# Moving the small steps of expert routing to other engines, and shifting attention's streams in the planned order

## The chip, the cores and the metric

The kernel runs on one core of a Trainium2 chip. The metric is device time in microseconds (us) of one execution, as the median of several runs. Besides, one execution is recorded by the hardware profiler; its busy times, waits and timelines are what this document reads.

Engines are named as in the profile: PE (TensorE), DVE (VectorE), ACT (ScalarE), POOL (GpSimd) and SP (SyncE, which issues most of the DMAs). [...]

## What is computed

Eight images (x is 8 x 512 x 256, the context 8 x 1024 x 192) go through two blocks. The first is a cross-attention whose scores keep the 32 largest of 1024 per row and head, followed by a state-space convolution with film modulation and a GELU MLP. The second is a mixture of experts: each token goes through a shared expert and through the one of 8 routed experts with the largest gate logit. Cut to what matters here:

```
scores = einsum('bthd,bghd->bhtg', Q, K) / sqrt(DH)
topv, topi = top_k(scores, 32)
attn = zeros.at[..., topi].set(softmax(topv)); attn_mean = attn.mean(axis=1)
c_t = attn_mean @ V            # feeds film, the convolution, the MLP
...
logits = x @ gate_w
top_val = max(logits); top_id = argmax(logits)
xs = x * sigmoid(top_val)
y = silu(xs @ rt_gate[e]) * (xs @ rt_up[e]) @ rt_down[e]   # e = top_id
out = swiglu(x, sh_gate, sh_up, sh_down) + y
```

## The kernel before, in words

**Streams.** The work of each image b is written as generators. `prepare(b)` (line 434) loads x and the context, normalises, and makes the transposed keys and queries kT and qT. `attention` (905) is one generator over all images: 64 steps, each one 128-row tile and two heads. `scores` (890) multiplies queries and keys on PE into PSUM and copies the result on ACT into two `sc` tiles (pool pq, four buffers, so two steps' worth); it is called one step ahead. A step then makes pairwise maxima and minima (`mn`, on DVE and POOL), finds the 32nd largest by repeated MAX8 and MATCH_REPLACE8 on DVE, takes Exp on ACT, masks on DVE, and sums heads into `acc` on POOL. After four heads `weighted` (872) transposes acc on PE (`pa`) and multiplies with the context (`pu`) into uT. `mixed(b)` (1053) does film and convolution (xm, pxf, yf, py, xr); `after_mix(b)` (1095) does the MLP (pm, ga, am), the norms, routing, and the shared expert (p, sg, ge, ae). `routed` runs routed-expert blocks of 128 rows (xb, pg, pu, ger, pyr), loading the weights of the expert that a block belongs to. While attention of image b runs, `behind(b - 1)` (1365) runs the rest of image b - 1, with the routed blocks of image b - 2 in it, and `prepare(b + 1)` runs too. Image 7's own rest, with 15 routed blocks, has no attention beside it.

**Routing** (1150 to 1184, once per image). The gate logits `lg` are copied from PSUM; DVE finds the largest (mx) and its index (ix) for each of four row tiles. The index is cast to a float (fx) and compared with iota8 to a one-hot oh (128 x 4 x 8). A row's place within its expert's table is the count of earlier rows of that expert. `cum`, 128 x 5 x 8, carries running one-hot sums: four dependent additions per image. Two small matmuls into one PSUM bank, before16 (a strict triangle of ones) by oh and ones16 by cum, give the ranks pw; pw times oh summed over experts, plus fx times CAP, is the row number, cast to ix_, and four indirect DMAs on POOL's queue scatter the rows into a table in DRAM (xtab). The sigmoid of the largest logit (sg_) scales the rows on ACT before that.

**blocks_of** (1213, images 1 to 7) turns counts into a list of (expert, first row) of blocks that are full: a matmul of ones16 by cum (pcnt), then some twenty tiny DVE operations on 128 x 8 tiles (nb, pre, base, di, pdone, cm, rd) up to the integer list `blk`, which SP's queue reads before it loads a block's weights. In the last image it lists all that remain.

**The order.** All calls go through a planner (class Plan). `note` and `time` give each operation a cost in us; `add` (179) numbers it and sets its priority `op.k = op.i - self.lead` in line 181 (a smaller k goes first); `order` (218) simulates the five engines and always issues, on the engine that can begin first, the available operation with the smallest k. Whatever comes out is the fixed order of each engine's queue. `ahead` (307) runs one step of a generator with `lead` set: LEAD_A for attention, LEAD_P for preparation, both 0. Where the plan has PE idle, `busy` (1394) puts in filler matmuls, `idle`.

## Time and profile before

| | |
|---|---|
| runs | 1898.41 us median of 3 (1895.82 to 1899.57) |
| profiled execution | 1896.74 us, span of instructions 1895.0 us |
| granted TensorE clock | 0.949 |
| busy: PE, DVE, ACT, POOL | 1727.0, 1483.8, 1187.0, 1043.7 us |
| PE filler matmuls `idle` | 397.2 us, 1574 of them |
| first `mn` of images 1 to 7 | 287.6, 465.8, 649.6, 835.5, 1024.4, 1221.2, 1418.7 us |
| last masked product of attention on DVE | ends at 1621.4 us |

How to read the lines: a group or timeline line names start and duration (us), engine, source line, operation and `output<-inputs` with shapes. Nearly every operation has line L324, the planner's issue line, so one goes by tile names. A table of stretches gives the stretch, its length, then for PE, weight loads, DVE, ACT and POOL the busy us with the count in brackets, then the granted clock, the DMA share and GB/s. A line of waits gives the waiting engine and tile, what released it, the total in us, the number of times and the longest. The strips cut the span into 40 slices; each digit is busy tenths.

### The profile page before, as it was taken

The numbers are of one execution on the slowest core, as the hardware profiler recorded it, in microseconds if no ns is written. First come the engines' busy times: TensorE is split into PE (matmuls) and PEld (weight loads), VectorE is DVE, ScalarE is ACT, GpSimd is POOL, SyncE is SP. The second block draws the span as 40 slices with busy tenths as digits, with TensorE's granted clock in tenths as the row PEclk, the third lists the DMA queues.
The fourth block names the chain that finished last, engine by engine and source line by source line (L and its number), as shares of the span: only waits on it lengthen the run. The fifth ranks groups of instructions, "written<-read, shape, count | busy, mean of one in ns | idle before, by whom it ended". The sixth has DMA issues, their size and how long they took to land. (4 is left out here: it accounts for less than half of the span.)

```text
span 1895.0 us, 24257 instructions
## 1 busy us (share of the span) xinstructions
PE 1727.0 (91%) x7913; PEld 998.3 (53%) x7913; DVE 1483.8 (78%) x2975; ACT 1187.0 (63%) x2022; POOL 1043.7 (55%) x916
## 2 busy tenths in 40 slices
PE   7598997989998999989899899989998999899996
PEld 3254443435543554556447453755465546657685
DVE  4999997897989899879998989888988999431210
ACT  6577753478757875977578657965696659513221
POOL 6454353665656657584655657465747665532122
PEclk9799997989989999989999899989998999999998
DMA  4000110001200120134004220323023302642594
GB/s 111 1 1 12 41 35 17 1 12 45 67 17 12 56 79 11 35 111 140 1 12 142 74 68 12 112 64 108 12 70 106 92 1 71 205 156 75 176 288 134
DMA packets 101302, 131.89 MB, mean 70 GB/s; under 512 B 9687, under 2 KB 73004, under 8 KB 101166
## 3 DMA queue, kind: packets, MB, share of 16 engines
q1 hardware_dynamic: 93102, 121.05, 20.8%
q0 software_dynamic: 7008, 8.42, 2.5%
q8 instruction: 65, 1.06, 0.2%
q10 hardware_dynamic: 1056, 0.79, 0.1%
q14 instruction: 71, 0.58, 0.1%
HBM read 112.22 MB, written 18.78 MB: 69 GB/s over the span
## 5 line engine op out<-in xcount | busy, mean ns | idle before, releaser
L1396 PE MATMUL idle<-ones 128*128 128x512 bf16 x1574 | 397.2, 397 | 0.0
L324 POOL TENSOR_TENSOR mn<-sc 128x512 int32<-128x512 int32 x128 | 203.1, 1600 | 223.6 <-DVE top L324 165.9
L324 POOL TENSOR_TENSOR acc<-acc,e 128x1024 f32<-128x1024 f32 x96 | 233.8, 2436 | 86.1 <-ACT e L324 80.1
L1396 PEld LDWEIGHTS <-ones 128*128 128x128 bf16 x1574 | 153.2, 102 | 238.8 <-issue 104.8
L324 DVE MAX8 top<-left 128x8 f32<-128x512 f32 x384 | 265.9, 692 | 11.3
L324 PE MATMUL pS<-kT,qT 32*128 32x512 f32 x512 | 199.6, 668 | 36.9 <-ACT sc L324 35.7
L324 DVE SCALAR_TENSOR_TENSOR e<-sc,t,e 128x1024 f32<-128x1024 f32 x128 | 215.9, 1709 | 10.7 <-ACT e L324 10.0
L324 POOL TENSOR_TENSOR mn<-mn 128x512 int32<-128x512 int32 x128 | 176.4, 1389 | 81.3 <-DVE mn L324 78.5
L324 ACT ACT_TABLE_LOAD x139 | 178.3, 1283 | 5.5 <-issue 2.0
L324 ACT COPY sc<-pS 128x512 f32<-128x512 f32 x256 | 140.3, 583 | 63.2 <-PE pS L324 62.0
L324 DVE MAX8 top<-mn 128x8 f32<-128x512 f32 x256 | 169.2, 678 | 10.6 <-POOL mn L324 10.5
L324 DVE MATCH_REPLACE8 left<-top,left 128x512 f32<-128x512 f32 x256 | 172.9, 676 | 0.0
L324 ACT ACTIVATE e<-sc,sm 128x1024 f32<-128x1024 f32 x128 | 147.0, 1149 | 8.8 <-POOL acc L324 3.9
L324 ACT ACTIVATE junk<-sc,sm 128x1024 bf16<-128x1024 f32 x128 | 146.1, 1142 | 1.6
L324 DVE TENSOR_TENSOR mn<-sc 128x512 f32<-128x512 f32 x128 | 117.3, 945 | 14.2 <-ACT sc L324 14.2
L324 PEld LDWEIGHTS pu<-aT,cx 128*96 128x96 f32 x1024 | 115.7, 163 | 16.2 <-ACT aT L324 7.0
L324 PE MATMUL pu<-aT,cx 128*96 128x128 f32 x1024 | 120.7, 273 | 3.7 <-ACT aT L324 2.8
L324 PE MATMUL am<-w,ga 128*128 128x256 f32 x512 | 117.9, 382 | 0.8 <-ACT ga L324 0.7
L324 PE MATMUL pm<-hT,w 128*128 128x512 f32 x256 | 117.9, 596 | 0.5 <-ACT hT L324 0.2
L324 PEld LDWEIGHTS pS<-kT,qT 32*128 32x128 f32 x512 | 56.9, 190 | 112.7 <-ACT sc L324 69.5
L324 POOL DMA_INDIRECT out_dram<-yb,to x38 | 65.9, 1735 | 84.8 <-DMA out_dram<-yb,to 47.7
L324 ACT ACTIVATE e<-e,sm 128x1024 f32<-128x1024 f32 x96 | 107.6, 1141 | 7.2 <-DVE sm L324 7.2
(266 smaller groups left out, 3153.1 us busy)
## 6 DMA issues: line engine op xcount, KB each, us to landing
rt_gate<-in_L_ffn_rt_gate_dram SPq DMA_DIRECT2D x38, 512.0 KB, 4.8
rt_up<-in_L_ffn_rt_up_dram SPq DMA_DIRECT2D x38, 512.0 KB, 3.7
rt_down<-in_L_ffn_rt_down_dram SPq DMA_DIRECT2D x38, 512.0 KB, 4.1
w<-in_L_xattn_W_dram SPq DMA_DIRECT2D x32, 512.0 KB, 4.3
cx<-in_ctx_dram SPq DMA_DIRECT2D x7, 768.0 KB
xtab<-zt SPq DMA_DIRECT2D x8, 642.5 KB, 4.8
xb<-xtab SPq DMA_DIRECT2D x38, 128.5 KB, 4.2
xt<-in_x_dram SPq DMA_DIRECT2D x8, 512.0 KB, 4.4
```

The lines of the kernel that those rows point to most:

```text
L324: o.fn()
L1396: nc.tensor.matmul(idle, ones16, bc(ones16, 1, 4), start=True, stop=True)
```

## The change

It does four things. (1) The planner's costs change: indirect DMAs on POOL 1.15 us, with accumulation 1.7 (both 1.1 before); ACT operations at least 0.24 us, and 0.16 more for 129 to 256 elements from SBUF. (2) Leads: attention and preparation get -100, and `scores` adds 150 while it notes its operations. (3) Routing's small operations go to an engine E: POOL for images 0 to 6, DVE for image 7. The cum chain goes: `cum` becomes 128 x 8 and holds only the total of earlier images; ranks come from five matmuls, before16 by oh, ones16 by oh shifted by one, two and three tiles, and ones16 by cum broadcast. DVE sums oh over tiles (om), and E adds that to cum. (4) In blocks_of the scaling of the counts is a copy from PSUM on ACT, and most other operations go to E; two multiply-adds become two instructions each, because the tile minimum, the comparison, the reduction and the final minimum alone stay on DVE.

```diff
--- before.py
+++ after.py
@@ -117,7 +117,7 @@
         if dma:
             moved = out if kw.get("out_offset") is None else kw["in_"]
             size = self.width(moved) * list(moved.shape)[0] * 4
-            op.cost = 1.1 if eng == "POOL" else 0.45
+            op.cost = 0.45 if eng != "POOL" else 1.7 if kw.get("compute_op") is not None else 1.15
             op.lat = (2.9 if "indirect" not in method else 2.4) + size / WIRE
             if kw.get("compute_op") is not None:
                 op.lat += 2.0
@@ -156,7 +156,9 @@
                 t = 0.07 + 0.0012 * width + (0.0 if psum else 0.1 + 0.0008 * width)
             return t, None
         if eng == "ACT":
-            t = max(0.2, 0.085 + 0.00104 * n) + (0.19 if len(outs) > 1 else 0)
+            t = max(0.24, 0.085 + 0.00104 * n) + (0.19 if len(outs) > 1 else 0)
+            if not psum and 128 < n <= 256:
+                t += 0.16
             f = args[2] if method == "activation" else None
             return t, (TABLES.get(str(f).split(".")[-1]) if f is not None else None)
         if eng == "POOL":
@@ -331,7 +333,8 @@
 SWITCH = 100
 WIRE = 350e3
 NPREP = 13
-LEAD_A, LEAD_P = 0, 0
+
+LEAD_A, LEAD_P, LEAD_S = -100, -100, 150
 BETWEEN = 3
 
 
@@ -541,7 +544,7 @@
     tid = const.tile([P, B * NT], I32, name="tid")
     xtab = dr.tile([NE * CAP + P, DX], F32, name="xtab")
 
-    cum = const.tile([P, NT + 1, NE], BF16, name="cum")
+    cum = const.tile([P, NE], BF16, name="cum")
     pdone = const.tile([P, NE], F32, name="pdone")
 
     pre = const.tile([P, 4, 2 * NE], F32, name="pre")
@@ -889,6 +892,7 @@
 
     def scores(b, s, t, h0):
 
+        plan.lead += LEAD_S
         n = f"{b}_{t}_{h0}"
         sc = [pq.tile([P, G], F32, tag="s", name=f"sc{n}_{i}") for i in range(2)]
         for q in range(G // 512):
@@ -900,6 +904,7 @@
                 TE.matmul(pS[i], s.qT[hp, t * P : (t + 1) * P], s.kT[hp, qs], start=True, stop=True)
             for i in range(2):
                 S.copy(sc[i][:, qs], pS[i])
+        plan.lead -= LEAD_S
         return sc
 
     def attention(states):
@@ -1150,38 +1155,43 @@
         for t in range(NT):
             V.max(mx[:, t, :], lg[:, t, :])
             V.max_index(ix[:, t, :], mx[:, t, :], lg[:, t, :])
-        fx = pk.tile([P, NT], F32, tag="fx", name=f"fx{b}", bufs=1)
-        V.tensor_copy(fx, ix[:, :, 0])
+
+        E = V if b == B - 1 else GP
+        fx = pk.tile([P, 2, NT], F32, tag="fx", name=f"fx{b}", bufs=1)
+        E.tensor_copy(fx[:, 0], ix[:, :, 0])
         sg_ = pk.tile([P, NT], F32, tag="sg_", name=f"sgm{b}", bufs=1)
         S.activation(sg_, mx[:, :, 0], AF.Exp, scale=-1.0)
-        V.tensor_scalar(sg_, sg_, 1.0, None, ALU.add)
+        E.tensor_scalar(sg_, sg_, 1.0, None, ALU.add)
         V.reciprocal(sg_, sg_)
 
         oh = pk.tile([P, NT, NE], BF16, tag="oh", name=f"oh{b}", bufs=1)
-        cu = cum
-        V.tensor_tensor(oh, bc(iota8, 1, NT), bc(fx, 2, NE), ALU.is_equal)
-        for t in range(NT):
-            V.tensor_add(cu[:, t + 1, :], cu[:, t, :], oh[:, t, :])
+        V.tensor_tensor(oh, bc(iota8, 1, NT), bc(fx[:, 0], 2, NE), ALU.is_equal)
+        E.tensor_scalar(fx[:, 1], fx[:, 0], float(CAP), None, ALU.mult)
+
         pw = bank(f"pw{b}")
         oh2 = oh.rearrange("p t e -> p (t e)")
         TE.matmul(pw[:, : NT * NE], before16, oh2, start=True, stop=False)
-        TE.matmul(pw[:, : NT * NE], ones16, cu[:, :NT, :].rearrange("p t e -> p (t e)"),
-                  start=False, stop=True)
+        for t in range(1, NT):
+            TE.matmul(pw[:, t * NE : NT * NE], ones16, oh2[:, : (NT - t) * NE], start=False, stop=False,
+                      skip_group_check=True)
+        TE.matmul(pw[:, : NT * NE], ones16, bc(cum, 1, NT), start=False, stop=True)
         rk = pk.tile([P, NT, NE], F32, tag="rk", name=f"rk{b}", bufs=1)
         V.tensor_mul(rk, pw[:, : NT * NE].rearrange("p (t e) -> p t e", e=NE), oh)
-        rn = pk.tile([P, 2, NT], F32, tag="rn", name=f"rn{b}", bufs=1)
-        V.tensor_reduce(rn[:, 0], rk, AX.X, ALU.add)
-        V.scalar_tensor_tensor(rn[:, 1], fx, float(CAP), rn[:, 0], ALU.mult, ALU.add)
+        rn = pk.tile([P, NT], F32, tag="rn", name=f"rn{b}", bufs=1)
+        V.tensor_reduce(rn, rk, AX.X, ALU.add)
         ix_ = pk.tile([P, NT], I32, tag="ix_", name=f"row{b}")
-        V.tensor_copy(ix_, rn[:, 1])
-        V.tensor_copy(cu[:, 0, :], cu[:, NT, :])
+        E.tensor_add(rn, fx[:, 1], rn)
+        E.tensor_copy(ix_, rn)
+        om = pk.tile([P, NE], F32, tag="om", name=f"om{b}", bufs=1)
+        V.tensor_reduce(om, oh.rearrange("p t e -> p e t"), AX.X, ALU.add)
+        E.tensor_add(cum, cum, om)
         for t in range(NT):
             S.activation(hd[:, t, :], hd[:, t, :], AF.Copy, scale=sg_[:, t : t + 1])
         for t in range(NT):
             GP.indirect_dma_start(out=xtab[:], out_offset=bass.IndirectOffsetOnAxis(ap=ix_[:, t : t + 1], axis=0),
                                   in_=hx[:, t, :], in_offset=None)
         if b in TAKE and not general:
-            blocks_of(blk[b], TAKE[b], b == B - 1)
+            blocks_of(E, blk[b], TAKE[b], b == B - 1)
         yield
 
         acc = accs(f"ae{b}")
@@ -1210,33 +1220,36 @@
         yield
 
 
-    def blocks_of(to, n, all_):
+    def blocks_of(E, to, n, all_):
 
         pc = bank(f"pcnt_{to.name}")
-        TE.matmul(pc[:, :NE], ones16, cum[:, NT, :], start=True, stop=True)
-        w_ = pk.tile([P, 3, NE], F32, tag="bw", name=f"bw_{to.name}", bufs=1)
+        TE.matmul(pc[:, :NE], ones16, cum, start=True, stop=True)
+        w_ = pk.tile([P, 2, NE], F32, tag="bw", name=f"bw_{to.name}", bufs=1)
         nb, di = w_[:, 0, :], w_[:, 1, :]
-        V.tensor_scalar(nb, pc[:, :NE], 63.5 if all_ else -63.5, 1.0 / P, ALU.add, ALU.mult)
-        V.tensor_scalar(nb, nb, MAGIC, MAGIC, ALU.add, ALU.subtract)
-        V.tensor_sub(pre[:, 0, NE:], nb, pdone)
+        S.activation(nb, pc[:, :NE], AF.Copy, scale=1.0 / P)
+        E.tensor_scalar(nb, nb, (63.5 if all_ else -63.5) / P, MAGIC, ALU.add, ALU.add)
+        E.tensor_scalar(nb, nb, MAGIC, None, ALU.subtract)
+        E.tensor_sub(pre[:, 0, NE:], nb, pdone)
         for i in range(3):
-            V.tensor_add(pre[:, i + 1, NE:], pre[:, i, NE:], pre[:, i, NE - 2 ** i : 2 * NE - 2 ** i])
+            E.tensor_add(pre[:, i + 1, NE:], pre[:, i, NE:], pre[:, i, NE - 2 ** i : 2 * NE - 2 ** i])
         en, st = pre[:, 3, NE:], pre[:, 3, NE - 1 : 2 * NE - 1]
         if all_:
             V.tensor_scalar(few, en[:, NE - 1 :], float(n), None, ALU.is_le)
         V.tensor_scalar(en, en, float(n), None, ALU.min)
 
-        V.tensor_sub(base[:, :NE], pdone, st)
-        V.scalar_tensor_tensor(base[:, :NE], base[:, :NE], float(P), capse, ALU.mult, ALU.add)
-        V.tensor_sub(di, base[:, 1:], base[:, :NE])
-        V.tensor_sub(nb, en, st)
-        V.tensor_add(pdone, pdone, nb)
+        E.tensor_sub(base[:, :NE], pdone, st)
+        E.tensor_scalar(base[:, :NE], base[:, :NE], float(P), None, ALU.mult)
+        E.tensor_add(base[:, :NE], base[:, :NE], capse)
+        E.tensor_sub(di, base[:, 1:], base[:, :NE])
+        E.tensor_sub(nb, en, st)
+        E.tensor_add(pdone, pdone, nb)
         cm = pk.tile([P, 2, n, NE], F32, tag="t2", name=f"cm_{to.name}")
         V.tensor_tensor(cm[:, 0], bc(iotab[:, :n], 2, NE), bc(en, 1, n), ALU.is_ge)
-        V.tensor_mul(cm[:, 1], cm[:, 0], bc(di, 1, n))
+        E.tensor_mul(cm[:, 1], cm[:, 0], bc(di, 1, n))
         rd = pk.tile([P, 2, n], F32, tag="rd", name=f"rd_{to.name}", bufs=1)
         V.tensor_reduce(rd, cm, AX.X, ALU.add)
-        V.scalar_tensor_tensor(rd[:, 1], rd[:, 1], base[:, 0:1], iotap[:, :n], ALU.add, ALU.add)
+        E.tensor_scalar(rd[:, 1], rd[:, 1], base[:, 0:1], None, ALU.add)
+        E.tensor_add(rd[:, 1], rd[:, 1], iotap[:, :n])
         V.tensor_tensor(to, rd, blim[:, :, :n], ALU.min)
 
     def cleared():
@@ -1244,7 +1257,7 @@
 
 
         pc = bank("pfree")
-        TE.matmul(pc[:, :NE], ones16, cum[:, 0, :], start=True, stop=True)
+        TE.matmul(pc[:, :NE], ones16, cum, start=True, stop=True)
         V.tensor_tensor(free, capse, pc[:, :NE], ALU.add)
         n = NT + 1
         zt = pk.tile([P, n, DX], F32, tag="cx", name="zt")
@@ -1428,7 +1441,7 @@
             together((mixed(b, s), n_mix))
             together((after_mix(b, s), n_mlp))
         blks = const.tile([P, 2, NBLK], I32, name="blks")
-        blocks_of(blks, NBLK, True)
+        blocks_of(V, blks, NBLK, True)
         for i in range(NBLK):
             with tc.block():
                 block(blks, i, f"g_{i}")()
```

## The prediction

> **What bounds the kernel now.** I read the page's engine totals and its 40 slices first, because the chain that ended last holds only the 0.1% after the last scatter and says nothing of the rest.
>
> ```profile
> PE 1727.0 (91%) x7913; PEld 998.3 (53%) x7913; DVE 1483.8 (78%) x2975; ACT 1187.0 (63%) x2022; POOL 1043.7 (55%) x916
> ...
> DVE  4999997897989899879998989888988999431210
> POOL 6454353665656657584655657465747665532122
> ```
>
> PE looks fullest, but its largest group is `idle`, 1574 filler matmuls of 397.2 us: its real work is 1727 - 397 = 1330 us. VectorE (DVE) stands at eight or nine tenths until slice 34 (about 1615 us) and then falls: that is where attention ends. So there are two regimes, and the table of 50 us stretches shows how they alternate within one image (about 197 us):
>
> ```profile
> 1000.00:1050.00 50.00, 47.93 (x285) 36.47 (x284) 37.95 (x86) 41.20 (x66) 30.96 (x30) 1.00 0.45 135
> 1050.00:1100.00 50.00, 45.99 (x175) 26.68 (x175) 48.01 (x107) 34.01 (x55) 25.65 (x23) 0.90 0.39 108
> 1100.00:1150.00 50.00, 45.34 (x150) 22.27 (x149) 41.61 (x75) 24.25 (x42) 32.66 (x25) 0.93 0.10 27
> 1150.00:1200.00 50.00, 48.92 (x201) 25.65 (x200) 48.73 (x95) 43.02 (x82) 33.17 (x29) 0.97 0.08 22
> ```
>
> Third busy figure: DVE, 176.3 of 200 us (88%). In the first stretch (MLP and routed experts) PE leads and DVE idles 12 us; in the second and fourth DVE has no room. So a microsecond taken from DVE there is worth nearly a microsecond. Next, the waits of DVE from 850 to 1640 us:
>
> ```profile
> DVE xr L324 <- PE am L324: 15.5, 3, 5.2
> DVE xm L324 <- PE pfi L324: 12.8, 8, 4.1
> DVE top L324 <- POOL mn L324: 7.7, 3, 2.7
> ...
> DVE mn L324 <- ACT sc L324: 4.5, 4, 1.8
> ```
>
> Few and short: the order on paper mostly holds. The first two are places where PE came later than planned. Then the DVE timeline over one routing:
>
> ```profile
> 1051.96 3.40 DVE L324 CAST fx<-ix 128x4 f32<-128x4 uint32 x1
> ...
> 1055.62 0.75 DVE L324 TENSOR_TENSOR cum<-cum,oh 128x8 bf16<-128x8 bf16 x4
> ...
> 1059.99 3.01 DVE L324 TENSOR_SCALAR pre<-pre 128x8 f32<-128x8 f32 x1
> ...
> 1063.24 2.20 DVE L324 SCALAR_TENSOR_TENSOR base<-base,capse 128x8 f32<-128x8 f32 x1
> ```
>
> and POOL beside it:
>
> ```profile
> 1052.04 3.29 POOL L324 TENSOR_TENSOR xo<-xo,bout 128x256 f32<-128x256 f32 x4
> ...
> 1060.61 4.80 POOL L324 TENSOR_TENSOR acc<-acc,e 128x1024 f32<-128x1024 f32 x2
> ```
>
> Four numbers per partition take DVE 3.40 us, ending with POOL's adds at 1055.3. The routing runs from 1050.24 to 1066.85, 16.6 us; in image 7, where POOL is idle, the same steps take 7.8 us. Last, the end of attention on POOL and PE:
>
> ```profile
> 1633.91 2.92 POOL L324 TENSOR_TENSOR acc<-acc,e 128x1024 f32<-128x1024 f32 x1
> ```
> ```profile
> 1653.77 3.62 PE L324 MATMUL ae<-sh_down,ge 128*128 128x256 f32 x16
> 1657.22 1.04 PE L324 MATMUL pa<-ident,acc 128*128 128x128 f32 x8
> ```
>
> The last attention tile is ready at 1636.8 us, and its transposes (`pa`) wait 20 us behind image 6's shared experts, though all of image 7's 238 us tail hangs on them.
>
> **What the Trainium skill says.** "SBUF — State Buffer", Who interferes with whom: VectorE and GpSimd share a port pair; a VectorE cast or tensor_scalar in a two-port mode, or an instruction with two SBUF inputs against a GpSimd read, locks out or is locked out for the whole instruction. The trace agrees: 3.40, 3.01, 2.20 us where the same instructions take 0.17 alone. "Perfetto Trace Analysis", Optimizing Scalar/DVE Operations, warns that offloading between these two engines might not help for that reason; here what moves is tiny and the waits are DVE's, so I expect most of it to help. The same page, GPSIMD Engine Instruction, calls POOL spans unreliable, so POOL prices below are rough.
>
> **The change, part by part.**
>
> *A. Routing off DVE.* Removed from DVE, summed over images from the rows of the page by shape, less image 7's short ones where it keeps them: fx cast 8.5; base multiply-add 7.1; rank multiply-add 2.9; cum adds, all 32, 7.2, and cum copy 1.3; sigmoid's add 1.1; row cast 1.1; blocks_of's two scalings 1.1 + 1.0; its subtract and adds into pre 1.0 + 3.4; base, di, nb, pdone 4.1; cm multiply 1.1; rd add 1.3. Sum 42.2 us. Added to DVE: om reduction 8 x 0.19 = 1.5, image 7's split steps about 1.1. Net 39.6. Of it 17 us is waiting for the port (fx 7.3, base 6.1, cum 2.1, rank 1.8 above their undisturbed times). Such waiting can move to the next DVE instruction that reads two tensors, so I count half: 22.6 + 8.5 = **31 us**, ends 10 (only part of it falls where DVE has no room) and 40. It lies on the path: in that stretch PE waited 3.9 us for `ge` and ACT 4.5 us for `sgm`. The `pre` minimum, 9.9 us over seven, stays on DVE.
>
> What takes it over: POOL gets 7 x 6 + 6 x 15 = 132 small instructions at 0.34 us (va and rs_e rows, 337 and 339 ns) = 45 us, to 57% of its span; cover is its idle time, and uncovered it would cost up to 45. PE gets 8 x 3 = 24 more small matmuls at 0.18 us (pw rows), 4.3 us, in place of fillers. ACT gets seven PSUM copies at about 0.2 us (sm row, 204 ns), 1.4 us. PE's ranks no longer wait for the cum chain (1.4 us): counted zero.
>
> *B. Order.* The diff lowers the priority of attention and preparation by 100 operation numbers and raises scores by 150 over the rest of attention, so 50 ahead of everything else. DVE 2975, ACT 1883, POOL 916 and half of PE's 6339 real matmuls make 8940 operations; most fall before 1640 us, so about 5.4 per us: 100 numbers are 18 us, 50 are 9. MLP, mixing and routing then take DVE, ACT and PE first, and attention becomes filler that may lag in the DVE-full stretches and catch up in the PE-full ones, fed by scores sent early. The sc buffers stay four, two steps of 25.6 us. Its direct target is DVE's waits for scores and minima, over the whole page 14.2 (mn on sc) + 10.5 (top on mn) = 24.7; I take half, **12 us**. The 12 us of DVE idle in each PE-full stretch could also fill: five such stretches, up to 60; I count none of it but keep 30 as the good end. The bad end is a loss of 10. Preparation 18 us later stays hidden: qT is ready 37 to 53 us before its image's first `mn`. Planner costs of POOL DMAs become 1.7 and 1.15 (trace 1735 and 1135 ns) and of 256-wide ACT operations about 0.51 (trace 495 to 592): truer, no direct time.
>
> *C. End of attention.* Image 6's remaining work runs up to 18 us earlier against attention, so less of the 20 us in front of the last `pa` is left; DVE's share of it (7.6 us routing, some ge) then delays attention. 20 - 8 = **12 us**, ends 0 and 20.
>
> *D. New waits.* In six images DVE meets POOL five times (oh after fx; reciprocal after the add; minimum after pre; reduction after the cm product; the block list after rd), in image 0 twice: 32 meetings. Queued behind the waiting DVE instruction is attention's top-k; behind PE's pcnt, which now waits for POOL's cum, are the shared experts' matmuls; behind ACT's copy of the counts are Exp and evictions. POOL's own queue has 2.4 us acc adds ahead of a small step. Before, DVE's 27 waits for POOL (mn, xr, yf) took 24.4 us, 0.9 each; most meetings never wait, so I take 0.4: **+12 us**, ends 0 and 75. Scatter rows come later on POOL's queue, but their readers are 100 us away. Block lists likewise: `blk` at 1066.85, first used by PE near 1215. Image 7 stays on DVE: without four cum adds (0.75) and a copy, with om, a cum add, an ACT hop, three split steps: about **+1 us** in front of the last 15 blocks' weight loads, uncovered because DMA is then 95% busy.
>
> Sum: -31 - 12 - 12 + 12 + 1 = -42. The profiled execution took 1896.7 us (span 1895.0), so 1854.7; the median of the three runs is 1.7 us higher: **1856 us**.
>
> **Rivals.** *Catch-up works fully:* attention also fills the PE-full stretches, 30 us more, and A comes whole: about 1818. For it: 12 us idle in each. Against: sc holds two steps, and DVE at 91% is already high. *Savings swallowed:* the port waits return and DVE idles where it worked: A gives 10, B nothing, C 4: -14 + 13, no change to -15, about 1888. For it: DVE and POOL share the port. *Slower, by meetings:* if POOL runs behind the plan by one acc add, 2.4 us, at each of the 32 meetings, D is 77 instead of 12: -42 + 65 = +23, **1921**. It decides from (42 + 12) / 32 = 1.7 us per meeting. For it: queues run in a fixed order and POOL's small steps vary from 0.2 to 1.1 us. Against: POOL is idle 45% of the time and before was the waiting side (165.9 us of mn on top). That the change does nothing would need DVE not to matter, which the slices contradict.
>
> **From cases to numbers.** Forecast (1828 to 1878) 0.55; full catch-up (below 1828) 0.15; swallowed (1878 to 1894) 0.12; within 0.2% of before (about what a measurement of this kernel can tell from no change) 0.05; slower 0.13. Faster 0.82, same 0.05, slower 0.13. The range 1800 to 1897 leaves out the slower case, some of "same" and the far end of catch-up.
>
> **What would show it.** A: DVE busy 1435 to 1450, no fx or cum adds, POOL near 1090, `pre` minimum shorter. B: DVE in the first of each image's stretches above 38 of 50, fewer waits for sc and am. C: less than 10 us between the last acc and its `pa`. D: DVE waits for fx, sgm, pre, cm, rd below 15 us together. The prediction is wrong if these waits pass 50 us, if image intervals stay at 197 us although DVE's busy time fell, or if attention ends later than 1600.

## The result, and the profile after

The kernel after takes 1882.95 us (median; 1871.4 to 1897.77) beside 1896.6 us for the kernel before on the same chip: ratio 0.9943, 95% interval 0.9926 to 0.9959. That is 13.65 us less, where 42 had been forecast. The sign holds and the time lies inside the range, but the size is a third of the forecast. The profiled execution (span 1875.8 us, before 1895.0) is one of the quicker ones: twelve of the 20 took 1871 to 1884 us at a granted clock of 0.952 to 0.959, eight took 1891 to 1898 at 0.948 to 0.951, and which of the two follows the other isn't shown; so its 19 us must not be read as the worth of the change.

The page of the kernel after, engine totals and strips:

```profile
PE 1712.8 (91%) x7888; PEld 992.7 (53%) x7888; DVE 1465.7 (78%) x2841; ACT 1173.7 (63%) x2020; POOL 1089.6 (58%) x1048
...
DVE  4999988898889887989778989788998999531210
POOL 5454435665765665577655856585758677532122
```

POOL took the 45 us that were forecast. DVE lost only 18 of 40 us, and its strip has 15 nines in place of 19. The four 50 us stretches, kernel after (columns: window, length, busy us of PE, PEld, DVE, ACT, POOL, granted clock, DMA share, GB/s):

```profile
1000.00:1050.00 50.00, 47.12 (x291) 35.17 (x290) 42.10 (x99) 44.07 (x75) 37.60 (x39) 1.00 0.48 127
1050.00:1100.00 50.00, 41.68 (x168) 24.99 (x168) 47.08 (x81) 33.46 (x52) 34.17 (x40) 0.97 0.43 127
1100.00:1150.00 50.00, 48.39 (x161) 22.84 (x162) 42.26 (x84) 25.04 (x43) 31.25 (x28) 0.97 0.05 16
1150.00:1200.00 50.00, 47.34 (x165) 25.08 (x164) 43.33 (x80) 40.18 (x74) 29.00 (x24) 0.93 0.04 11
```

The first stretch rose from 37.95 to 42.10 us of DVE, as the earlier scores were to do; the fourth fell from 48.73 to 43.33. DVE is not fuller (174.8 us in the four, before 176.3), it is filled at other times. Its waits from 850 to 1640 us, kernel after (us in total, times, longest):

```profile
DVE xm L326 <- PE pfi L326: 28.6, 12, 6.5
DVE e L326 <- ACT e L326: 16.0, 5, 9.5
DVE mn L326 <- ACT sc L326: 9.6, 4, 3.4
DVE pre L326 <- POOL pre L326: 8.1, 4, 4.0
```

The wait for the film products `pfi` has grown from 12.8 to 28.6 us and that for `sc` from 4.5 to 9.6; those for the MLP's products `am` (15.5 us before) and for POOL's half of `mn` (7.7 us) are no longer among the long ones. `pre` is a new meeting of the two engines. The timeline of one routing on DVE, kernel after:

```profile
1047.10 0.18 DVE L326 RECIPROCAL sgm<-sgm 128x4 f32<-128x4 f32 x1
1047.19 0.18 DVE L326 TENSOR_TENSOR oh<-iota,fx 128x32 bf16<-128x32 f32 x1
...
1047.53 2.82 DVE L326 TENSOR_TENSOR mn<-sc 128x512 f32<-128x512 f32 x1
...
1056.10 1.23 DVE L326 TENSOR_SCALAR pre<-pre 128x8 f32<-128x8 f32 x1 [0.40 <-POOL pre L326]
...
1063.21 0.17 DVE L326 TENSOR_TENSOR blk<-rd_blk,blim 128x8 int32<-128x8 f32 x1 [0.49 <-POOL rd_blk L326]
```

and on POOL beside it:

```profile
1044.93 0.88 POOL L326 CAST fx<-ix 128x4 f32<-128x4 uint32 x1
...
1047.45 2.36 POOL L326 TENSOR_TENSOR acc<-acc,e 128x1024 f32<-128x1024 f32 x1
...
1051.84 1.09 POOL L326 DMA_INDIRECT xtab<-hd,row  x1 [0.56 <-POOL row L326]
...
1057.47 1.09 POOL L326 DMA_INDIRECT xtab<-hd,row  x1 [0.17 <-issue]
...
1061.56 1.33 POOL L326 TENSOR_SCALAR rd_blk<-rd_blk,base 128x4 f32<-128x4 f32 x1
```

The tiny steps are gone from DVE, but its `mn` maximum (0.67 us when undisturbed) took 2.82 us and ended 0.5 us after POOL's 2.36 us attention sum, which had begun just before it: the lock-out that the Trainium skill describes ("SBUF — State Buffer", Who interferes with whom) has met another instruction. POOL's steps stand in one queue with its own scatters, 1.09 us each. The end of attention, on POOL and then on PE, kernel after:

```profile
1622.27 2.35 POOL L326 TENSOR_TENSOR acc<-acc,e 128x1024 f32<-128x1024 f32 x1
```
```profile
1628.85 0.38 PE L326 MATMUL pa<-ident,acc 128*128 128x128 f32 x2
...
1642.74 0.66 PE L326 MATMUL pxb<-ident,xb 128*128 128x128 f32 x2 [3.67 <-DMA xb<-xtab]
...
1644.04 1.91 PE L326 MATMUL pfi<-wf,uT 97*128 97x512 f32 x2
```

From the last sum to its transposes `pa` it is 4 us now, not 20. But a routed block's `pxb`, waiting 3.67 us for rows from `xtab`, stands in front of image 7's last film products.

Two of the prediction's own signs of being wrong came true: attention ended later than 1600 us (1611.5), and the images follow each other hardly faster. From image 1's first `mn` to image 7's it is 187.5 us an image on average, before 189.2. (DVE makes 16 `mn` an image. The times that the table of the kernel before gives as first ones belong to the last step of the image before; counted through, images 1 to 7 begin at 302.4, 490.4, 679.7, 871.2, 1043.1, 1240.0 and 1437.5 us, so the preparation of images 2 to 7, `qT`, is ready 61 us or more before its use, not 37 to 53.)

### The profile page after: what moved, and what is told of

It reads as the page before. It is cut to its first block, busy times and chain, and to the rows that moved or that the text cites. A ratio compares the mean times of both kernels' runs of the same rounds, so it can differ in the third digit from the quotient of the medians.

```text
span 1875.8 us, 24133 instructions
## 1 busy us (share of the span) xinstructions
PE 1712.8 (91%) x7888; PEld 992.7 (53%) x7888; DVE 1465.7 (78%) x2841; ACT 1173.7 (63%) x2020; POOL 1089.6 (58%) x1048
## 5 line engine op out<-in xcount | busy, mean ns | idle before, releaser
L1409 PE MATMUL idle<-ones 128*128 128x512 bf16 x1525 | 380.7, 392 | 0.0
L1409 PEld LDWEIGHTS <-ones 128*128 128x128 bf16 x1525 | 149.2, 101 | 197.6 <-issue 64.7
L326 DVE SCALAR_TENSOR_TENSOR e<-sc,t,e 128x1024 f32<-128x1024 f32 x128 | 210.3, 1660 | 18.2 <-ACT e L326 18.2
L326 PE MATMUL pS<-kT,qT 32*128 32x512 f32 x512 | 209.7, 663 | 13.9 <-ACT sc L326 13.4
L326 POOL TENSOR_TENSOR mn<-mn 128x512 int32<-128x512 int32 x128 | 180.8, 1424 | 64.7 <-DVE mn L326 61.4
L326 DVE TENSOR_TENSOR mn<-sc 128x512 f32<-128x512 f32 x128 | 150.1, 1198 | 24.8 <-ACT sc L326 24.8
L326 PE MATMUL pu<-aT,cx 128*96 128x128 f32 x1024 | 131.1, 277 | 0.9 <-ACT aT L326 0.9
L326 PEld LDWEIGHTS pu<-aT,cx 128*96 128x96 f32 x1024 | 119.5, 165 | 21.9 <-issue 15.2
```

The costliest lines, as they stand in the source:

```text
L326: o.fn()
L1409: nc.tensor.matmul(idle, ones16, bc(ones16, 1, 4), start=True, stop=True)
```

## Two numbers that divide a span

The experiments are read by two numbers from each trace: when the last masked product of attention ends on DVE (the last `e<-sc,t,e`), and what is left of the span after it. In the kernel before these are 1621.4 and 273.6 us, in the kernel after 1611.5 and 264.3. I call them attention and rest. Each trace is of one execution, and the executions of one kernel differ (those of the kernel after by 26 us), so a few microseconds between two traces say little.

The theories: **P**, the port waiting taken from the small steps comes back at `mn` and the other large products; **W**, DVE's busy time isn't what sets the pace; **K**, the planner's dearer prices ate the gain; **F**, the idle fillers keep PE from catching up; **L**, the luck of one written order is as large as the effect. The last one is needed since every edit makes the planner write a new order for all engines.

## Experiments: one part at a time

**No leads, `mn` ahead too, routing on VectorE.** Three edits of the kernel after:

```diff
-LEAD_A, LEAD_P, LEAD_S = -100, -100, 150
+LEAD_A, LEAD_P, LEAD_S = 0, 0, 0
```


> The changed kernel with all three leads at 0: routing off VectorE and the new costs stay, the shift of the streams goes. Theory P (the shared port: the shift puts the maxima mn on DVE beside POOL's acc adds, and mn grew from 117 to 150 us): mn falls back to 115 to 125, DVE busy to about 1440, and the time is below the changed kernel's, ratio to before about 0.985. Rival W (DVE's busy time is no longer the limit in the middle; what was gained came from the shift of the streams and shows at the end of attention): ratio 0.998 to 1.003 although DVE's busy time falls by some 40.

Measured: 1899.55 us, ratio 1.0024 [1.0010, 1.0037]. DVE's busy time fell to 1450.5 us, and nothing was gained, as W had it.

```diff
+                plan.lead += LEAD_S
                 V.tensor_tensor(m_[:, 0], lo, hi, ALU.max)
...
+                plan.lead -= LEAD_S
```


> The changed kernel with the maxima and minima mn of a step (two on DVE, four on POOL) given the same lead of 150 as its scores, so that they stand before the step before's masked products and its acc adds. Theory P: mn on DVE falls from 150 to below 125, DVE busy to about 1440, ratio to before 0.978 to 0.987. Rival W: mn falls likewise but the time stays at 0.992 to 0.997.

Measured: 1931.19 us, 1.0169 [1.0143, 1.0195]; `mn` did not get shorter (153.5 us in all), and attention ended at 1677.5 us. Neither theory had this: more of the lead is worse.

```diff
-        E = V if b == B - 1 else GP
+        E = V
```


> The changed kernel with E on VectorE for every image: the new ranks, costs and leads stay, routing's small steps are back on DVE. Theory P (a microsecond of DVE counts): DVE busy 1490 to 1500, ratio to before 1.003 to 1.012. Rival W: ratio 0.992 to 0.998, the offload is worth nothing. Rival M (DVE waiting for POOL at the handovers ate the offload): faster than the changed kernel, below 0.992.

Measured: 1896.48 us, 0.9991 [0.9976, 1.0005]. None of the three forecasts holds. Beside the leads the move to GpSimd was worth 0.5% in this order (0.9943 against 0.9991), though without the leads and with the same prices the whole new routing was worth nothing (1.0024 above; the prices alone, below, 1.0019).

**The leads alone**, put into the kernel before (prices and routing as before):

```diff
-LEAD_A, LEAD_P = 0, 0
+LEAD_A, LEAD_P, LEAD_S = -100, -100, 150
...
+        plan.lead += LEAD_S
         n = f"{b}_{t}_{h0}"
...
+        plan.lead -= LEAD_S
         return sc
```


> The kernel before with the three leads alone. Theory P: mn at about 150, DVE busy at 1510 to 1520, the last pa still some 20 us earlier against the end of attention, ratio 0.998 to 1.010. Rival W: the gain is the shift's, ratio 0.992 to 0.995 as in the changed kernel.

Measured: 1902.64 us, 1.0034 [1.0017, 1.0051]. DVE's waits up to the end of attention, first in the kernel before:

```profile
DVE xm L324 <- PE pfi L324: 29.2, 11, 8.7
DVE xr L324 <- PE am L324: 20.4, 4, 5.2
DVE mn L324 <- ACT sc L324: 14.2, 10, 2.4
...
DVE top L324 <- POOL mn L324: 10.5, 7, 2.7
DVE e L324 <- ACT e L324: 10.0, 9, 3.2
```

and in the kernel before with the leads alone:

```profile
DVE xm L324 <- PE pfi L324: 65.7, 18, 11.5
...
DVE mn L324 <- ACT sc L324: 5.6, 6, 2.7
...
DVE top L324 <- POOL mn L324: 1.1, 1, 1.1
...
DVE xr L324 <- PE am L324: 0.4, 1, 0.4
```

The group of `mn` maxima over the whole run (busy us, mean ns, idle before), in the kernel before and with the leads alone:

```profile
L324 DVE TENSOR_TENSOR mn<-sc 128x512 f32<-128x512 f32 x128 | 117.3, 945 | 14.2 <-ACT sc L324 14.2
```
```profile
L324 DVE TENSOR_TENSOR mn<-sc 128x512 f32<-128x512 f32 x128 | 132.4, 1058 | 5.6 <-ACT sc L324 5.6
```

This is the price of the leads. The scores do come earlier: the waits for `sc` and for POOL's `mn` fall by 18 us, more than the 12 that step B took, and the one for `am` by 20. But the wait for film products more than doubles (+36.5 us), several others grow, and all of DVE's waits up to the end of attention come to 187.8 us against 155.6. The `mn` maxima take 15 us longer, but other DVE work gets shorter: its busy time there rose by 4.5 us only. Attention ends at 1655.8 us, 34 later; the rest is 247.6 us, 26 shorter. The time itself (1.0034) is within P's range and not W's. The leads move work from behind attention to in front of its end, and pay for it.

**The prices, apart and with the other parts.**

```diff
-            op.cost = 1.1 if eng == "POOL" else 0.45
+            op.cost = 0.45 if eng != "POOL" else 1.7 if kw.get("compute_op") is not None else 1.15
...
-            t = max(0.2, 0.085 + 0.00104 * n) + (0.19 if len(outs) > 1 else 0)
+            t = max(0.24, 0.085 + 0.00104 * n) + (0.19 if len(outs) > 1 else 0)
+            if not psum and 128 < n <= 256:
+                t += 0.16
```

That diff alone on the kernel before:


> The kernel before, with only the planner's two price edits (GpSimd's own transfers at 1.15 or 1.7 us, ScalarE's small copies dearer); no instruction is moved to another engine. The routing without the leads had gained nothing (1.0024), though VectorE was busy for 33 us less. Theory K: the dearer prices alone bring an order that is worse, and this ate the gain of the routing. The planner's own total for this order is 31 us longer than for the kernel before (1851 against 1820 us): 1912 to 1925 us, ratio 1.008 to 1.015. Rival W: VectorE's time is not what binds, and prices do little: 1890 to 1904 us, ratio 0.997 to 1.004.


Measured: 1900.77 us, 1.0019 [1.0009, 1.0029].

The new routing alone, that is the kernel after with this diff undone and all leads at zero:


> The new routing alone: the kernel after, with the old prices in the planner and all leads at zero. Theory K (the dearer prices ate the gain of the routing): the routing shows here, 1870 to 1885 us, ratio 0.986 to 0.994. Rival W (VectorE's time is not what binds, whatever the prices): 1892 to 1905 us, ratio 0.998 to 1.004, with VectorE's busy time near 1450 us and its idle time up by as much.


Measured: 1885.9 us, 0.9932 [0.9909, 0.9955].

The diff undone with the leads kept:


> The kernel after with the old prices, leads kept: what the price edits are worth in the company of the other parts. Theory K: without the dearer prices the kernel is faster than the kernel after, 1860 to 1875 us, ratio 0.981 to 0.989. Rival W: the prices are what makes the plan fit the chip beside moved work; without them it is slower than the kernel after, 1888 to 1900 us, ratio 0.995 to 1.002.


Measured: 1893.58 us, 0.9967 [0.9945, 0.9989].

K is right in one place only: without leads the prices cost the routing 0.9% (1.0024 against 0.9932). Alone they cost 0.2%, and beside the leads they gain 0.2% (0.9943 against 0.9967). Such a pattern gives no price of a part: either the parts act on each other, or L holds.

**Where the routing's 38 us go.** In the run with the routing alone DVE was busy for 1391.3 us up to the end of attention, against 1425.3 before: 34.0 less. Attention ended at 1603.9 us, 17.5 earlier. Its waits up to there, routing alone:

```profile
DVE mn L324 <- ACT sc L324: 24.4, 12, 5.3
DVE e L324 <- ACT e L324: 24.0, 9, 6.7
```

Before, these two came to 14.2 and 10.0 us. So 24 of the 34 us were met by waiting for ScalarE's copies of the scores and its exponentials (all of DVE's waits there rose by 20.9 us, to 176.5). In these 48.4 us ScalarE was itself at work for 42.7, 9 of them loading function tables, so it was not merely passing on a wait of its own. The pair of orders with the price 0.30, further below, shows the same: 33.8 us less busy, the two waits 49.0 us in place of 19.1, attention 11.2 us earlier. P's place for the loss is nearly empty: `mn` took 116.8 us in all against 117.3, and though the comparison `oh` took 7.2 us in place of 1.5, DVE's busy time over the whole run fell by 37.7 of the 39.6 us forecast as net. About half the saving ran into ScalarE, the next limit. The rest of the span grew from 273.6 to 280.5 us. Image 6's routing shows why, on DVE, in the kernel before and with the routing alone:

```profile
1634.46 0.19 DVE L324 COPY lg<-pg 128x32 f32<-128x32 f32 x1 [4.43 <-PE pg L324]
...
1642.07 0.17 DVE L324 TENSOR_TENSOR blk<-rd_blk,blim 128x8 int32<-128x8 f32 x1
```

```profile
1618.21 0.19 DVE L324 COPY lg<-pg 128x32 f32<-128x32 f32 x1 [4.43 <-PE pg L324]
...
1629.39 0.22 DVE L324 TENSOR_REDUCE rd_blk<-cm_blk 128x8 f32<-128x64 f32 x1 [1.36 <-POOL cm_blk L324]
1630.34 0.17 DVE L324 TENSOR_TENSOR blk<-rd_blk,blim 128x8 int32<-128x8 f32 x1 [0.73 <-POOL rd_blk L324]
```

and on POOL, routing alone:

```profile
1623.14 1.08 POOL L324 DMA_INDIRECT xtab<-hd,row  x1 [0.56 <-POOL row L324]
1624.30 0.59 POOL L324 TENSOR_SCALAR bw_blk<-bw_blk 128x8 f32<-128x8 f32 x2
...
1627.56 1.07 POOL L324 DMA_INDIRECT xtab<-hd,row  x1 [0.15 <-issue]
1628.66 0.21 POOL L324 TENSOR_TENSOR bw_blk<-pre 128x8 f32<-128x8 f32 x1
```

From `lg` to the block list `blk` it is 12.1 us, in the kernel before 7.6 us at the same place (no attention sums disturb DVE there any more). Two scatters of 1.08 us are in the queue between the small steps. The list is followed by the fetch of `xb` and `pxb`, and by what PE has queued behind that; image 7's last film products `pxf` begin 59.5 us after the end of attention, against 54.7.

## Experiments: fillers

The fillers are put in behind the planner, so in this section the order of all other instructions stays the same.

The kernel after with half the fillers:

```diff
-FILL_MAX, FILL, STEP = 12.0, 0.85, 0.22
+FILL_MAX, FILL, STEP = 12.0, 0.45, 0.22
```


> The kernel after with the idle fillers on TensorE cut by half (they fill 0.45 of each planned gap in place of 0.85; some 800 in place of 1525). Theory F: the fillers stand in TensorE's queue ahead of the film's and the gates' products, so that once TensorE is behind the plan it cannot catch up, and that is why VectorE's wait for the film's product has grown to 54.5 us: with half of them the wait falls under 40 us and the time is 1860 to 1875 us, ratio 0.981 to 0.989. Rival: the fillers hold TensorE's granted clock up, and with fewer it falls under 0.92: every product is longer, and the time is 1890 to 1915 us, ratio 0.996 to 1.010.


Measured: 1874.67 us, 0.9877 [0.9845, 0.9909], the fastest kernel of this study. But the wait for film products fell only from 54.5 to 49.3 us over the run, and the clock fell to 0.912, so F is not shown by it. The two profiled executions differ by 1.9 us only (1875.8 and 1873.9), so the traces don't show where the gain lies.

The same diff in the kernel before:


> The kernel before with the idle fillers on TensorE cut as in the run that did so with the kernel after (0.45 of each planned gap in place of 0.85). That run went from 0.9943 to 0.9877. Theory F (the fillers in TensorE's queue keep it from catching up, and eat what the change gives): the kernel before, which has little to catch up on (it runs 77 us behind its plan, the kernel after 107 us), gains little, 1888 to 1897 us, ratio 0.995 to 1.000, and the change is worth 0.8 to 1.2 per cent where fillers are few. Rival G (fewer fillers are worth the same 0.7 per cent to any version): 1878 to 1887 us, ratio 0.990 to 0.995, and the change is worth 0.6 per cent in both.


Measured: 1905.55 us, 1.0056 [1.0036, 1.0076]; both expectations miss. The clocks of the two, kernel after with half the fillers first:

```profile
core 0: 1873.9 us, clock 0.912
```
```profile
core 0: 1903.8 us, clock 0.899
```

The kernel before loses its time early: image 1's first `mn` begins at 313.3 us in place of 302.4, in the kernel after at 305.7 in place of 304.2. The stretch from 100 to 200 us with half the fillers, kernel before and then kernel after (both had a clock of 0.97 there with all fillers):

```profile
100.00:200.00 100.00, 78.72 (x536) 46.85 (x537) 90.02 (x119) 69.61 (x106) 46.15 (x29) 0.74 0.02 6
```
```profile
100.00:200.00 100.00, 72.01 (x486) 37.54 (x484) 96.33 (x118) 75.01 (x118) 52.62 (x32) 0.82 0.04 11
```

The kernel that loses has the lower clock there; that this is the cause isn't shown.

The same diff with the routing alone:


> The new routing alone (old prices, no leads), with the fillers cut by half. The routing alone took VectorE's busy time down by 38 us and the time by 11 us (0.9932). Theory F: with room in TensorE's queue more of the 38 us comes through: 1855 to 1872 us, ratio 0.978 to 0.987. Rival W (one image's chain of meetings between ScalarE, VectorE and GpSimd sets the pace, and neither VectorE's time nor TensorE's is what binds): the two gains add up at most, 1872 to 1885 us, ratio 0.987 to 0.994.


Measured: 1885.76 us, 0.9965 [0.9951, 0.9978]; both miss.

The kernel after with none (`FILL` at 0.0):


> The kernel after with no idle fillers at all in the planned part (some of TensorE's warm-up stays). Theory F carried to its end: TensorE can always catch up, VectorE's wait for the film's product falls under 35 us; but the granted clock, which was 0.955 with 1525 fillers and 0.912 with 751, falls to near 0.87, and TensorE's own products (1332 us at 0.955) take some 130 us more. If the lost clock stays hidden in TensorE's gaps: 1855 to 1872 us, ratio 0.978 to 0.987. If it comes onto the path: 1880 to 1910 us, ratio 0.991 to 1.007.


Measured: 1910.41 us, 1.0105 [1.0063, 1.0147], clock 0.854, and the wait for film products still 56.5 us. F's forecast (under 35 us) falls. That the wait doesn't come from fillers at all is not shown, since at this clock TensorE's own products take longer too (1505 us in place of 1332). Why the kernel after gains by half the fillers and the kernel before loses is open.

## Experiments: the luck of an order

One price, the signal from PE to another engine, was moved by 0.02 us. No instruction, engine or lead changes; the written order does, in some places.

```diff
-HOP = {"PE": 0.28, "DVE": 0.15, "ACT": 0.22, "POOL": 0.18, "SP": 0.1, "DMA": 0.1}
+HOP = {"PE": 0.30, "DVE": 0.15, "ACT": 0.22, "POOL": 0.18, "SP": 0.1, "DMA": 0.1}
```

The kernel after with 0.30:


> The kernel after with one price of the planner moved by a trifle: the signal from TensorE to another engine at 0.30 in place of 0.28 us. No instruction, engine or lead is changed; only the order that the planner writes moves a little (its own total is 1779 against 1776 us). If the order's chance is small, this gives the kernel after again: 1879 to 1887 us, ratio 0.992 to 0.996. If parts of this size are within the luck of one order, it lands elsewhere by 0.3 per cent or more, 1865 to 1878 or 1888 to 1900 us, and a part that is worth less than that cannot be told from a new order.


Measured: 1896.64 us, 1.0025 [1.0007, 1.0042]. The whole gain is gone.

The kernel before with 0.30, and with 0.26:


> The kernel before with the planner's price of a signal from TensorE at 0.30 in place of 0.28 us; nothing but the order moves. Theory L (luck of an order is as large as the effect): off from the kernel before by 0.3 per cent or more, either way, ratio 0.990 to 0.997 or 1.003 to 1.010. Rival (the kernel before is insensitive, only the kernel after with its leads stands on a knife's edge): ratio 0.998 to 1.002.


Measured: 1895.18 us, 1.0016 [1.0004, 1.0027], inside the rival's range.


> The same with 0.26 us. Theory L: again off by 0.3 per cent or more, either way. Rival: ratio 0.998 to 1.002.


Measured: 1898.5 us, 1.0036 [1.0025, 1.0047], inside L's.

The kernel after with 0.26:


> The kernel after with the price at 0.26 us. Theory L: between 0.990 and 1.005, and the mean of the kernel after's orders (0.9943, 1.0025 and this) lies near 0.997, not below the mean of the kernel before's by more than 0.5 per cent. Rival (the result 0.9943 is the change's own worth, 1.0025 was an outlier): 0.992 to 0.996.


Measured: 1888.65 us, 0.9969 [0.9955, 0.9984], inside L's.

The routing alone with 0.30:


> The new routing alone (old prices, no leads) with the price at 0.30 us. Its first order gave 0.9932. If the routing is worth its 0.7 per cent whatever the order: 0.6 to 0.8 per cent below the kernel before with the same price. Theory L: somewhere between 0.985 and 1.003; over the three prices together the routing is worth 0.3 to 1.2 per cent, since its 38 us less on VectorE are in every order.


Measured: 1899.85 us, 1.0040 [1.0020, 1.0061], that is 0.2% above the kernel before with the same price, where with 0.28 it had been 0.7% below.

L holds for the kernel after and for the routing alone, where a new order moved the time by up to 0.8% and 1.1%; the kernel before moved by 0.4% at most. Three orders of the kernel before average 1.0017, three of the kernel after 0.9979, so the change is worth about 0.4% (7 us). With so few orders and such a spread, 0.4% can't be told from nothing: the 13.65 us are clear of the noise of one order only, and that order is the best of the three. The routing alone averages 0.9986 over two orders.

Two things are not shown. All five new orders were slower than the one with 0.28, so 0.28 may be a lucky price for these kernels. And each ratio has its own runs of the kernel before beside it (medians of 1891.6 to 1896.6 us), but the kernel after with 0.28 was timed on one occasion only, so a part of its distance from its other orders may belong to the occasion.

The two numbers of each trace (us):

| kernel | attention ends | rest of span |
|---|---|---|
| before, three orders | 1621.4, 1621.7, 1622.2 | 273.6, 275.4, 272.6 |
| routing alone, two orders | 1603.9, 1610.4 | 280.5, 281.1 |
| leads alone | 1655.8 | 247.6 |
| routing and leads, old prices | 1626.4 | 265.8 |
| after, three orders | 1611.5, 1627.9, 1608.7 | 264.3, 264.7, 266.1 |

The rest depends on the parts and hardly on luck. Attention's end is steady within 1 us in the kernel before, moves by 6.5 us with the new routing, and by 19 us with the leads too. How much of the 19 is the order and how much the execution that was profiled isn't shown.

## Experiments: a microsecond of VectorE in a fixed order

To keep luck out, 64 instructions were added that the planner doesn't see, so that the order stays the same:

```diff
+                if o.eng == "DVE" and o.what[1].startswith(("mx", "ix")):
+                    more()
...
+    def more():
+        nc.vector.tensor_reduce(mz, bc(ones, 1, 3), AX.X, ALU.add)
```

In the kernel before, then in the kernel after:


> The kernel before, its written order kept exactly, with one reduction over 384 elements more on VectorE after each of the routing's 64 row maxima and indices, on data of its own that nobody waits for: by the planner's price 0.53 us each, 34 us in all, 4.2 us an image. If a microsecond of VectorE is worth nearly a microsecond, as the prediction had it: 24 us or more, ratio 1.012 to 1.020. If VectorE has slack and waits take up most of it (theory W, with the orders' mean for the routing of 0.3 per cent for 38 us): 3 to 14 us, ratio 1.001 to 1.008.


Measured: 1922.8 us, 1.0141 [1.0119, 1.0162].


> The same 64 reductions in the kernel after, its order kept exactly. If VectorE's time is worth as much here as before, the same step up from its own 0.9943: 1.006 to 1.015 for a full price, 0.995 to 1.003 with slack. If the change has made slack on VectorE (it waits longer for TensorE and ScalarE than before, 177 against 163 us), its step is the smaller of the two.


Measured: 1906.4 us, 1.0062 [1.0036, 1.0088].

The added group in the kernel before:

```profile
L1403 DVE TENSOR_REDUCE mz<-ones 128x3 f32<-128x384 f32 x64 | 34.6, 541 | 0.0
```

and its share up to the end of attention and behind it (length, DVE busy us of this group alone and count, clock, DMA share, GB/s):

```profile
0.00:1635.80 1635.80, 25.95 (x48) 0.94 0.18 52
1635.80:1917.80 282.00, 8.65 (x16) 0.96 0.53 164
```

34.6 us more on DVE cost 0.0141 x 1894 = 26.7 us in the kernel before (0.77 a microsecond), and 0.0119 x 1894 = 22.5 us in the kernel after (0.65, by the difference of the two ratios, whose intervals leave 0.5 to 0.8). W in its plain form falls: DVE's time does count.

In the kernel before the two parts of the trace count differently. Up to the end of attention 25.9 us were added and it ended 14.3 us later (1635.8), 0.55 a microsecond, or 0.68 if the 3.2 us by which this execution lay under its median belong there; behind it 8.65 us were added and the rest grew by 8.4 us. Taking away 34.0 us up to the end of attention had brought 17.5, 0.51 a microsecond. So in these single traces a microsecond up to the end of attention is worth half to two thirds, whether it is added or taken away, and an added one behind it a whole one. What made the routing alone worth so little in all is that it also lengthened the rest.

## Why the prediction was right or wrong

Means over the orders in the table, on spans (before 1895.6 us, routing alone 1888.0, after 1881.1), put beside the steps. A and D meet in the attention of the routing alone; its rest is the routing's chain at the end; what the leads and prices add to both numbers is B and C.

The last column is an estimate that puts right which executions were profiled: it takes the rest from the traces, where it is steady, and the whole from the mean ratios of the medians (1.0017, 0.9986, 0.9979 of some 1895 us).

| step | forecast, us | traces, us | by medians, us |
|---|---|---|---|
| A and D: routing, up to the end of attention | -31 + 12 = -19 | 1607.2 - 1621.8 = -14.6 | -12.8 |
| D, end: the routing's chain behind attention | +1 | 280.8 - 273.9 = +6.9 | +6.9 |
| B: order, up to the end of attention | -12 | 1616.0 - 1607.2 = +8.8 | +14.5 |
| C: order, behind attention | -12 | 265.0 - 280.8 = -15.8 | -15.8 |
| sum | -42 | -14.7 | -7.2 |

The profiled executions of the kernel after were 2 to 12 us quicker than their medians; that the traces' sum lies near the 13.65 us of the first order is chance. The numbers up to the end of attention carry the luck of the few orders, several microseconds; B's differs from the forecast by more than that.

**B failed**, and it is the largest part of what is missing: 21 of 27 us by the traces, 26 of 35 by the medians. The prediction said that scores sent early would let attention catch up in PE's full stretches, and took half of the waits for `sc` and for POOL's `mn` as gain. In the leads alone these waits did fall (24.7 to 6.7 us). Put at nothing was what holding attention's other steps back costs: film products came later (29.2 to 65.7 us of waiting), and attention ended 34 us later in place of 12 earlier. Added to the routing at the old prices the leads cost 19 us there (1626.4 against 1607.2). At the new prices the mean of the kernel after is 6 us below the order without leads (1616.0 against 1622.0), half of the forecast, but there the profiled executions lay 7 us below and 4 us above their medians. The bad end that the step allowed, 10 us, was too small for the leads alone. That the loss comes through the film products is read from the waits; no run moved these products alone. Where the prediction looked for DVE at over 38 of 50 us in the first stretch of an image, 42.10 were found; it was a sign of moved work, not of gained time.

**A was nearly right in sum, with its parts wrong, and only at the old prices.** It had counted half the 17 us of port waiting as lost to the next instruction, and nearly a microsecond for each microsecond saved. In the routing alone hardly any of that waiting came back in sum (37.7 of 39.6 us came off DVE); instead 24 us of waiting for ScalarE came up. At the new prices without leads the routing brought nothing (1.0024 against 1.0019), in one order each. In the kernel after, `mn` did grow (150.1 us), but it also reached 131.7 us with the prices alone and 132.4 with the leads alone, so the order can bring this without the routing. The Trainium skill's warning about moving work between these two engines ("Perfetto Trace Analysis", Optimizing Scalar/DVE Operations) agrees in outcome only: DVE did get free, the freed time met another wait.

**D** had 12 us for meetings with POOL. In the kernel after DVE waited 8.1 us for `pre`, 2.6 for `cm`, 2.2 for `rd` and 0.7 for the sigmoid: 13.6 us of waiting, close to the 12, and the slower case, which decided at 1.7 us for each of 32 meetings, was far off. The 1 us for the end was too little: there every step is on the path, and POOL's scatters stand between them.

**C was right in its own number**: from the last sum to `pa` 4 us in place of 20, and 15.8 us off the rest of the span, though a wait of 3.67 us for `xb` now stands in the way. But B and C are two sides of one shift, as the leads alone show (34 us more before the end of attention, 26 less behind it), and the prediction summed them as two gains.

The case of swallowed savings (1888 us) came nearest to what happened: DVE idled where it had worked, though for ScalarE and the film products more than by port waits that returned. Its chance was set too low, because a step of unknown sign (B) was summed as a gain. That the first order landed at 1882.95 us and not nearer 1890 was, as far as three orders can tell, luck.

## What to carry to other kernels

A lead in a planned order moves work; count what is held back as well as what comes early. Before the parts of a change below one per cent are explained, move a price of the planner by a trifle and see how far the time goes; test the worth of an engine's microsecond with the order fixed. Split the span before comparing what work added costs with what work removed brings: here a microsecond of DVE was worth half to two thirds of one up to the end of attention, and an added one behind it a whole one.

## What the runs showed of the hardware

The granted clock fell with the number of idle matmuls on PE, and the time didn't follow it one way: in the kernel after 1525 gave a clock of 0.955 and a ratio of 0.9943, 751 gave 0.912 and 0.9877, none 0.854 and 1.0105. The same halving made the kernel before 0.6% slower. TensorE's own work took 1332 us (1712.8 - 380.7), 1402 us (1622.8 - 220.9) and 1505 us in these three; times the clock that is 1272, 1279 and 1285 us, so the lower clock accounts for nearly all of the stretch. With 751 the time fell in spite of 70 us more, so much of the stretch must have lain in PE's gaps.
